# A gated cross-attention block on one core: small per-partition instructions folded together, and a newly written order

## The chip, the cores and the metric

The kernel runs on one core of a Trainium2 chip. The metric is the device time of one execution in microseconds (us). Three executions of the kernel before took 279.45, 279.55 and 279.66 us, median 279.55 us.

The engines go by the names of the profile: PE multiplies matrices (PEld loads its weights), DVE, ACT and POOL work on vectors, and SP issues all the DMAs. Each engine takes its instructions strictly in the order in which the program gives them. An instruction whose input is missing holds up everything behind it on that engine.

## The reference, cut to what matters

Eight batches, x of 256 x 512 each, with a second input (`media`) of the same shape:

```python
x = x + tanh(g_xattn) * xattn(layernorm(x), media)
#   theta = theta_w @ media, phi = phi_w @ x, g = g_w @ x
#   t = softmax(theta.T @ phi) @ g
#   h = relu((t - mean(t)) * rsqrt(var(t) + 1e-5) * gamma + beta), mean and var over a whole batch
#   result: out_w @ h + media
x = x + tanh(g_ffn) * ffn(layernorm(x), w1, w2, w3)
#   bitlinear(a, w): a normalised by its root mean square (eps 1e-6), rounded to 8 bits per row
#                    (scale 127 / max|a|, max|a| at least 1e-5); w rounded to -1, 0, 1
#   h = silu(bitlinear(x, w1)) * bitlinear(x, w2);  result: bitlinear(h, w3)
```

The rows of a batch make two tiles of 128 x 512, so there are 16 feed-forward tiles; tile i belongs to batch i // 2. Each hidden row has 2048 numbers.

## The kernel before, in words

The program first collects 1512 steps, each with a label such as `ug3:0` (kind, part, batch or tile). A list `CFG["order"]` (line 68) then says in which order the steps are issued, and a table `CFG["alt"]` says which engine takes a step that could run on several. So the order on every engine, SP's DMA queue included, is written out in advance. A step waits for its inputs through semaphores, and a tile waits for a free buffer of its pool: 8 banks of PSUM, 31 buffers of 2 KB per partition, 7 of 4 KB and 7 of 8 KB.

The steps that this text speaks of:

- `Lx`, `Lm`, `wl`: loads of x, of media and of the fp32 weights (lines 203, 207, 283). `ws`, `wr`, `wq`: the weights' absolute sum, their scaling to int16 and their clipping to -1, 0, 1 (lines 296 to 321).
- Attention, per batch: `nr`, `np`, `nm`, `nx` normalise x (lines 347 to 352); `jtheta`, `jphi`, `jg` are projections on PE, `htheta`, `hphi` their copies out of PSUM; `sm` the scores, `sx` and `se` their maximum (DVE) and exponential (ACT); `ph`, `pl` split the softmax into two fp16 halves; `pt` transposes it by DMA; `av` multiplies it by g. `tw`, `tm`, `tu`, `td`, `tr`, `tp` make mean and reciprocal deviation of the result (lines 569 to 578). `rm` and `rx` add the media to x ahead of time (lines 444 to 451). `om` is the output projection and `oa` adds it to x, leaving the row sums in `osum` (line 621).
- Entry to the feed-forward part, `ffn_in`, per batch: `im` makes minus the mean out of `osum` (line 651), `iq` squares (ACT), `ir` takes the maximum, `iv`, `ie`, `ip`, `ic` turn these into scales, `iz` quantises x (line 667), `it` transposes the quantised batch by DMA into `fqt` (line 684). `ia`, `ib`, `if` and `ig` write the factors `fback` that take the quantisation back (lines 675 to 682).
- Feed-forward, per tile: `ug` and `uu` multiply `fqt` by w1 and w2, four blocks of four matmuls each (line 699); `us` is SiLU on ACT (line 709), `um` the product on DVE (line 711); `qs` and `qa` take sum of squares and maximum of the hidden row; `qf`, `qm`, `qc`, `qe`, `qr`, `qp`, `qb` are on one number per partition (lines 733 to 740); `qz` quantises the row and `qt` transposes it by DMA into `fhi`; `dm` multiplies by w3 and `da` adds to x. Batches 2 to 6 take a cheaper product of two by two blocks instead of `dm` (`tS`, `tP`, `tU`, `tA`, lines 826 to 897), with sums of weight blocks made once (`tW`).

Which step stands where decides much here. All 16 feed-forward blocks of batch 0 and those of batch 1 use the eight PSUM banks in turn with the attention of later batches, and `ug`/`uu` of batch 1 can't begin before `it:1` has landed.

Of the kernel before, what the change touches and what calls it, by code (L numbers as in the profile page):

```python
# [11 lines left out]
F16 = mybir.dt.float16  # L12
# [77 lines left out]
def flamingo_gated_block(  # L90
# [74 lines left out]


    xs = [[w_(f"x{b}_{c}", [P, T]) for c in range(DC)] for b in range(B)]
    meds = [[w_(f"med{b}_{c}", [P, T]) for c in range(DC)] for b in range(B)]
    proj_w = {n: c_(f"{n}_w", [P, DC, L]) for n in ("theta", "phi", "g")}
    proj_src = {"theta": theta_wT, "phi": phi_wT, "g": g_wT}  # L170

    cols, tg = c_("cols", [P, columns.shape[1]]), c_("tg", [P, 2])
    col = {n: (lambda k=k: cols()[:, k : k + 1]) for k, n in enumerate(("theta", "phi", "g"))}
    ob = lambda: cols()[:, 3 : 3 + DC]
    gates = lambda: cols()[:, 3 + DC : 5 + DC]
    gam, bet, ow = c_("gam", [P, T]), c_("bet", [P, T]), c_("ow", [P, D])
    ones, neg_half = c_("ones", [P, P]), c_("neg_half", [P, 2 * DC])

    fac = {n: (c_(f"{n}_max", [P, DC]), c_(f"{n}_sum", [P, 1]), c_(f"{n}_back", [P, 1]), c_(f"{n}_fwd", [P, 1])) for n in ("phi", "g")}
    half_w = {n: c_(f"{n}_half", [P, 2, DC, L], F16) for n in ("phi", "g")}  # L180
    theta_hi, theta_lo = c_("theta_whi", [P, DC, L], F32R), c_("theta_wlo", [P, DC, L], F32R)
    cols2 = c_("cols2", [P, 2])
    bias = {"theta": (lambda: cols2()[:, 0:1]), "phi": (lambda: cols2()[:, 1:2])}

    whole_x = [b for b in range(B) if b not in CFG["xsplit"]]
    whole_m = [b for b in range(B) if b not in CFG["msplit"]]
    assert set(whole_x) <= set(whole_m)
    keep = {"phi": False, "g": any(b not in CFG["p32"] for b in whole_x), "theta": any(b not in whole_x for b in whole_m)}
    scaled_t = {n: c_(f"{n}_sc", [P, DC, L]) if k else w_(f"{n}_sc", [P, 2 * DC, L]) for n, k in keep.items()}
# [19 lines left out]
    def constants():  # L209
        op("C:ones", lambda: V.memset(ones(), 1.0))  # L210
        op("C:half", lambda: V.memset(neg_half(), -0.5))
        if CFG["p32"] or CFG["rpe"]:
            op("C:id0", lambda: G.memset(ident(), 0.0))
            op(
                "C:id1",
                lambda: G.affine_select(
                    out=ident(), in_=ident(), compare_op=ALU.not_equal, fill=1.0, base=0, pattern=[[-1, P]], channel_multiplier=1
                ),
            )
        wps = ps_("warm")  # L220

        op("C:warm", lambda: [PE.matmul(wps()[:, 0:P], ones(), ones(), start=True, stop=True) for _ in range(CFG["warm"])])
        for n in ("theta", "phi", "g"):
            load_proj(n)
        op("Lc:0", lambda: nc.sync.dma_start(out=cols(), in_=columns))
        op("Lgam:0", lambda: nc.sync.dma_start(out=gam(), in_=ln_gamma))
        op("Lbet:0", lambda: nc.sync.dma_start(out=bet(), in_=ln_beta))
        op("Low:0", lambda: nc.sync.dma_start(out=ow(), in_=out_wT))
        op("C:tanh", lambda: S.activation(tg(), gates(), AF.Tanh))
        if CFG["rpe"]:  # L230
            tiny("C:gid", lambda e: e.tensor_scalar(gident(), ident(), tg()[:, 0:1], 1.0, ALU.mult, ALU.mult))

        tiny("C:ow", lambda e: e.tensor_scalar(ow(), ow(), tg()[:, 0:1], 1.0, ALU.mult, ALU.mult))
        op("C:owh", a=lambda: S.copy(ow_hi(), ow()), v=lambda: V.tensor_copy(ow_hi(), ow()))
        tiny("C:owl", lambda e: e.tensor_tensor(ow_lo(), ow(), ow_hi().bitcast(F32), ALU.subtract))
        tiny("C:ob", lambda e: e.tensor_scalar(ob(), ob(), tg()[:, 0:1], 1.0, ALU.mult, ALU.mult))

        for n in ("phi", "g"):
            mx, sm, back, fwd = fac[n]
            tot = ps_(f"{n}_tot")
            op(f"C:{n}max", lambda n=n, mx=mx: V.tensor_reduce(mx(), proj_w[n](), AX.X, ALU.max, apply_absolute_value=True))
            op(f"C:{n}sum", lambda mx=mx, sm=sm: V.tensor_reduce(sm(), mx(), AX.X, ALU.add))
            op(f"C:{n}tot", lambda sm=sm, tot=tot: PE.matmul(tot()[:, 0:1], ones(), sm(), start=True, stop=True))
            lim = 1e-30 if n == "phi" else 1e-2
            op(f"C:{n}back", lambda tot=tot, back=back, lim=lim: V.tensor_scalar(back(), tot()[:, 0:1], lim, 1.0 / G_SCALE, ALU.max, ALU.mult))
            op(f"C:{n}fwd", lambda back=back, fwd=fwd: V.reciprocal(fwd(), back()))
            tiny(f"C:{n}w", lambda e, n=n, fwd=fwd: e.tensor_scalar(scaled_w[n](), proj_w[n](), fwd(), 1.0, ALU.mult, ALU.mult))  # L250
            op(
                f"C:{n}h",
                a=lambda n=n: S.copy(half_w[n]()[:, 0], scaled_w[n]()),
                v=lambda n=n: V.tensor_copy(half_w[n]()[:, 0], scaled_w[n]()),
            )
            tiny(f"C:{n}l", lambda e, n=n: e.tensor_tensor(half_w[n]()[:, 1], scaled_w[n](), half_w[n]()[:, 0], ALU.subtract))
        pback, pfwd = fac["phi"][2:]
        tiny("C:tw", lambda e: e.tensor_scalar(scaled_w["theta"](), proj_w["theta"](), pback(), 1.0, ALU.mult, ALU.mult))
        tiny("C:tb", lambda e: e.tensor_scalar(cols2()[:, 0:1], col["theta"](), pback(), 1.0, ALU.mult, ALU.mult))
        tiny("C:pb", lambda e: e.tensor_scalar(cols2()[:, 1:2], col["phi"](), pfwd(), 1.0, ALU.mult, ALU.mult))  # L260
        op(
            "C:th",
            a=lambda: S.copy(theta_hi(), scaled_w["theta"]()),
            v=lambda: V.tensor_copy(theta_hi(), scaled_w["theta"]()),
        )
        tiny("C:tl", lambda e: e.tensor_tensor(theta_lo(), scaled_w["theta"](), theta_hi().bitcast(F32), ALU.subtract))
        tiny("C:gback2", lambda e: e.tensor_scalar(gback(), fac["g"][2](), 1.0 / P_SCALE, 1.0, ALU.mult, ALU.mult))
# [4 lines left out]
    def weights(n):  # L272
# [30 lines left out]
        if n < 2:  # L303
            op(f"wf:{n}", lambda: V.tensor_scalar(wfac()[:, n : n + 1], wmean()[:, n : n + 1], 1.0 / (127.0 * Q_UNIT), None, ALU.mult))
        else:
            op(f"wf:{n}", lambda: V.tensor_scalar(wmean()[:, 2:3], wmean()[:, 2:3], tg()[:, 1:2], None, ALU.mult))
# [22 lines left out]
    def attention(b):  # L329
# [215 lines left out]
        for g, pt in enumerate(pts):  # L545
# [14 lines left out]
        op(  # L560
            f"tx:{b}",
            a=lambda: S.activation(tx(), av(), AF.Identity, bias=col["g"](), scale=gb()),
            v=lambda: V.tensor_scalar(tx(), av(), gb(), col["g"](), ALU.mult, ALU.add),
        )
        op(f"tb:{b}", lambda: V.bn_stats(st(), tx()))
        op(f"ta:{b}", lambda: V.bn_aggr(mv2(), st()))
        op(
            f"tw:{b}",
            lambda: V.scalar_tensor_tensor(mv2()[:, 1:2], mv2()[:, 0:1], mv2()[:, 0:1], mv2()[:, 1:2], ALU.mult, ALU.add),
        )  # L570
        op(f"tm:{b}", lambda: PE.matmul(mps()[:, 0:2], ones(), mv2(), start=True, stop=True))
        op(f"tu:{b}", lambda: V.tensor_scalar(mu(), mps()[:, 0:2], 1.0 / P, None, ALU.mult))
        op(
            f"td:{b}",
            lambda: V.scalar_tensor_tensor(var(), mu()[:, 0:1], mu()[:, 0:1], mu()[:, 1:2], ALU.mult, ALU.subtract),
        )
        tiny(f"tr:{b}", lambda e: e.tensor_scalar(rs(), var(), -1.0, LN_EPS, ALU.mult, ALU.add))
        op(f"tp:{b}", lambda: G.tensor_tensor(rs(), rs(), neg_half()[:, 0:1], ALU.pow))
        h = tx
        op(f"hc:{b}", lambda: V.scalar_tensor_tensor(h(), tx(), mu()[:, 0:1], gam(), ALU.subtract, ALU.mult))  # L580
        op(f"hs:{b}", lambda: V.scalar_tensor_tensor(h(), h(), rs(), bet(), ALU.mult, ALU.add))
        if osp:
            hh, hl = w_(f"hh{b}", [P, T], F32R), w_(f"hl{b}", [P, T], F32R)
            op(
# [9 lines left out]
        else:  # L594
# [4 lines left out]
                p=lambda: G.tensor_scalar(h(), h(), 3e38, 0.0, ALU.min, ALU.max),  # L599
            )  # L600

        osums = sums[b] = []
        for c in range(DC):
            o = ps_(f"o_ps{b}_{c}")

# [193 lines left out]


    HC, HT = FC // 2, T // 2
    tw = w_("w3t", [P, 4, HC, HT], F8)

    def block(k, n, q):

# [154 lines left out]
```

## Time and profile before

| | before |
|---|---|
| three runs, median (lowest to highest) | 279.55 us (279.45 to 279.66) |
| the profiled execution: time, and its span from first to last instruction | 279.37 us, 277.6 us |
| granted PE clock, mean | 0.999 |
| PE busy | 271.3 us, 98% of the span |
| DVE, ACT, POOL busy | 254.0, 227.6, 205.9 us (91%, 82%, 74%) |
| DMA | 43.30 MB, mean 156 GB/s |

The span is the stretch that the trace covers; the other 1.8 us of the execution lie around it. A busy share is a mean over stages that differ: in some of them all four compute engines are busy at once. Matmuls overlap in PE, so that a matmul of 512 columns lasts 379 ns by itself but the next can start 216 ns later; a busy PE can still have steps that begin late, and these are found in the view of waits and in the timeline.

### The profile page before, as it was taken

How to read it: one execution, taken by the hardware profiler on the slowest of the kernel's cores; microseconds unless marked ns; L12 is line 12 of the kernel's file. 1: busy time of each engine (PE TensorE's matmuls, PEld its weight loads, DVE VectorE, ACT ScalarE, POOL GpSimd, SP SyncE). 2: the span in 40 equal slices, each digit the busy share in tenths (PEclk: the TensorE clock that was granted, in tenths of full speed). 3: DMA queues.
4: the chain of work that ended last, by engine and by line, in shares of the span. 5: the costliest groups of instructions: out<-in, count | busy, mean ns of one | idle time of the engine just before them, and what ended most of it. 6: DMA issues, size and time to landing. Idle time of an engine off the chain costs nothing.

```text
span 277.6 us, 4741 instructions
## 1 busy us (share of the span) xinstructions
PE 271.3 (98%) x1574; PEld 166.9 (60%) x1574; DVE 254.0 (91%) x537; ACT 227.6 (82%) x337; POOL 205.9 (74%) x273
## 2 busy tenths in 40 slices
PE   7999999999899999999999999999999999999995
PEld 7458585564365555545754778655545566457863
DVE  3798988999999989989999899997999889999895
ACT  1399999999989999899999899895867789675910
POOL 2588774799999998867896989758785855873461
PEclk9999999999999999999999999999999999999999
DMA  7999979998761325134948815916372356605685
GB/s 217 357 347 374 387 277 367 184 195 327 154 115 38 79 41 110 40 76 130 155 97 180 161 41 113 154 34 118 88 142 76 61 130 113 151 2 110 77 211 212
DMA packets 81528, 43.30 MB, mean 156 GB/s; under 512 B 67936, under 2 KB 69088, under 8 KB 81504
## 3 DMA queue, kind: packets, MB, share of 16 engines
q1 hardware_dynamic: 81504, 43.00, 62.2%
q8 instruction: 12, 0.20, 0.3%
q14 instruction: 12, 0.10, 0.1%
HBM read 22.02 MB, written 4.19 MB: 94 GB/s over the span
## 4 chain that ended last, share of the span: by engine, by line
PE 82%; DVE 8%; ACT 3%; issue 2%; DMA 2%; POOL 1%; SPq 0%; POOLq 0%; ACTq 0%
PE fup L699 18%; PE fgp L699 17%; PE dp L857 10%; PE fop L772 6%; PE av L538 4%; PE sc L463 4%; PE phi_ps L385 4%; PE theta_ps L385 3%; PE gx_ps L416 3%; PE tp L498 3%; PE o_ps L610 3%; PE sc L461 3%; PE av L551 3%; DVE nmax L472 2%; DMA med<-in_media 2%
## 5 line engine op out<-in xcount | busy, mean ns | idle before, releaser
L699 PEld LDWEIGHTS <-fqt 128*128 128x128 f16 x512 | 49.0, 99 | 56.8 <-issue 3.2
L699 PE MATMUL fgp<-w1q,fqt 128*128 128x512 f16 x256 | 61.7, 379 | 1.4 <-ACT fh L709 1.4
L699 PE MATMUL fup<-w2q,fqt 128*128 128x512 f16 x256 | 62.3, 379 | 0.0
L709 ACT ACTIVATE fh<-fgp,fback 128x512 f32<-128x512 f32 x64 | 41.1, 687 | 10.4 <-PE fgp L699 8.9
L711 DVE TENSOR_TENSOR fh<-fup,fh 128x512 f32<-128x512 f32 x64 | 42.6, 681 | 2.8 <-PE fup L699 1.6
L732 DVE TENSOR_REDUCE fham<-fh 128x1 f32<-128x2048 f32 x15 | 34.2, 2280 | 0.1
L731 ACT ACTIVATE fhq<-fh 128x2048 bf16<-128x2048 f32 x15 | 28.7, 1913 | 0.4 <-POOL fhfl L733 0.4
L745 ACT ACTIVATE fhq<-fh,fhqs 128x2048 f16<-128x2048 f32 (+1 forms) x14 | 26.6, 1907 | 1.9 <-DVE fhqs L735 1.7
L475 ACT ACTIVATE e<-sc,nmax 128x512 f32<-128x512 f32 x32 | 21.8, 689 | 2.8 <-DVE nmax L472 2.3
L772 PE MATMUL fop<-w3q,fhi 128*128 128x512 fp8e4 (+1 forms) x112 | 22.9, 349 | 0.0
L472 DVE TENSOR_REDUCE nmax<-sc 128x1 f32<-128x512 f32 x32 | 21.6, 681 | 0.7 <-PE sc L463 0.3
L450 POOL TENSOR_TENSOR x<-x,med 128x512 f32<-128x512 f32 x14 | 19.3, 1375 | 3.8 <-ACT med L444 3.7
L519 DVE SCALAR_TENSOR_TENSOR ph<-e,rden,ph 128x512 f16<-128x512 f32 x24 | 17.8, 760 | 0.0
L857 PEld LDWEIGHTS <-fhi 128*128 128x128 f16 x160 | 15.6, 98 | 3.6
L538 PE MATMUL av<-pt,gx 128*128 128x256 f16 x144 | 17.5, 273 | 0.0
L772 PEld LDWEIGHTS <-fhi 128*128 128x128 f16 x112 | 10.6, 98 | 9.3 <-DMA fhi<-fhq 0.4
L538 PEld LDWEIGHTS <-gx 128*128 128x128 f16 x144 | 13.8, 98 | 3.4 <-issue 0.3
L667 POOL TENSOR_SCALAR fq<-x,fnmu,fqs 128x512 f16<-128x512 f32 x16 | 14.1, 889 | 0.8 <-DVE fqs L663 0.2
L654 ACT ACTIVATE fsq<-x,fnmu 128x512 f32<-128x512 f32 x16 | 11.5, 719 | 3.1 <-DVE fnmu L651 2.3
L345 DVE BATCH_NORM_STATS2 bst<-x 128x6 f32<-128x512 f32 x16 | 10.8, 683 | 3.3 <-DMA x<-in_x 3.2
L416 PEld LDWEIGHTS <-xh 128*128 128x128 f16 x144 | 9.4, 98 | 5.5 <-issue 3.3
L621 DVE SCALAR_TENSOR_TENSOR x<-o_ps,x 128x512 f32<-128x512 f32 x16 | 10.9, 687 | 1.9 <-PE o_ps L610 1.6
(223 smaller groups left out, 688.9 us busy)
## 6 DMA issues: line engine op xcount, KB each, us to landing
x<-in_x SPq DMA_DIRECT2D x16, 256.0 KB, 4.0
med<-in_media SPq DMA_DIRECT2D x16, 256.0 KB, 4.5
w<-in_w2T SPq DMA_DIRECT2D x4, 1024.0 KB, 7.7
w<-in_w1T SPq DMA_DIRECT2D x4, 1024.0 KB, 8.2
w<-in_w3T SPq DMA_DIRECT2D x4, 1024.0 KB, 9.7
out<-x SPq DMA_DIRECT2D x15, 256.0 KB, 2.3
fhi<-fhq SPq DMA_TRANSPOSE x17, 4.4
gam<-in_ln_gamma SPq DMA_DIRECT2D x1, 256.0 KB, 10.4
```

What stands on the lines that cost most here:

```text
L385: PE.matmul(ps(), w, v, start=c == 0 and k == 0, stop=c == DC - 1 and k == e)
L472: op(f"sx{t}:{b}", lambda sc=sc, nmax=nmax: V.tensor_reduce(nmax(), sc(), AX.X, ALU.max, negate=True))
L475: lambda t=t, sc=sc, nmax=nmax, e=e: S.activation(e(), sc(), AF.Exp, bias=nmax(), accum_out=den()[:, t : t + 1]),
L538: PE.matmul(av()[:, ts(g, TG * P)], gx()[:, hg, ts(s, L)], v[:, hp, s], start=k == 0, stop=k == 3 * TCH - 1)
L699: PE.matmul(ps(), qt()[:, c * EC + k, :], wq[n][j]()[:, k, :], start=k == 0, stop=k == EC - 1)
L709: lambda j=j, gp=gp: S.activation(h()[:, ts(j, 512)], gp(), AF.Silu, scale=back()[:, c, 0:1]),
L711: op(f"um{j}:{i}", lambda j=j, up=up: V.tensor_tensor(h()[:, ts(j, 512)], up(), h()[:, ts(j, 512)], ALU.mult))
L731: op(f"qs:{i}", lambda: S.activation(hq().bitcast(BF16), h(), AF.Square, accum_out=ss()[:, 0:1]))
L732: op(f"qa:{i}", lambda: V.tensor_reduce(am()[:, 0:1], h(), AX.X, ALU.max, apply_absolute_value=True))
L745: return S.mul(hq()[:, sl], h()[:, sl], qs())
L772: PE.matmul(o()[:, sl], hi()[:, f, :], wq[2][f // 4]()[:, f % 4, sl], start=f == 0, stop=f == FC - 1)
L857: PE.matmul(banks[n]()[:, h * HT : (h + 1) * HT], l()[:, f, :], r(f), start=f == 0, stop=f == HC - 1)
```

## The change

Three things change together.

First, the small instructions. The variance's `tr` goes: `tu` adds 1e-5 to the second moment as it comes out of PSUM, from a constant `eps2`, and `td` subtracts the other way round. The two `osum` tiles of a batch become one with two columns, so that one `im` of two columns takes the place of two of one column. The two `if` become one with broadcast operands. `qf` goes, since its constant is put into `wfac`, the factor of the second weight; `qe` goes, since a new step `ge` of two columns per batch writes that value into a fourth column of `fback`. That is 8 `tr`, 8 `im`, 8 `if`, 16 `qf` and 16 `qe` less, and 8 `ge` and two small fills (`C:e0`, `C:e1`) more: 46 steps fewer, 1466 in all.

Second, `CFG["order"]` and `CFG["alt"]` are new throughout. PE and SP have the same 369 and 105 steps in another order. Between DVE, ACT and POOL, 126 steps change their engine: 48 leave DVE and 52 come to it, 23 leave ACT and 17 come, 55 leave POOL and 57 come. PE now issues all 16 blocks of batch 0 before the first of batch 1, where 13 stood ahead of it. The steps on POOL between `it:0`'s and `it:1`'s quantisation are now `wr1:0, im:1, wr0:0, rm0:2, np:4, rx0:2, rm1:3, ph0:3, ip:1, rm0:3, mh1:5, ic:1, iz0:1, iz1:1`; they were `im0:1, nr:4, ia:0, wr0:0, ib:0, wr1:0, rx0:2, rm1:3, np:4, ip:1, ic:1, iz0:1, iz1:1`.

Third, a second layout of the sums of weight blocks is added, for a setting that neither kernel uses.

```diff
-_upd(CFG, {..., "alt": {...}, "order": [0, 4, 2, 110, ...]})
+_upd(CFG, {..., "alt": {...}, "order": [...]})
...
+        op("C:e0", lambda: G.memset(eps2(), 0.0))
+        op("C:e1", lambda: G.memset(eps2()[:, 1:2], LN_EPS))
...
+            unit = 1.0 / (127.0 * Q_UNIT) / (Q_EPS * RMS_EPS**0.5 if n else 1.0)
+            op(f"wf:{n}", lambda: V.tensor_scalar(wfac()[:, n : n + 1], wmean()[:, n : n + 1], unit, None, ALU.mult))
...
-        op(f"tu:{b}", lambda: V.tensor_scalar(mu(), mps()[:, 0:2], 1.0 / P, None, ALU.mult))
+        op(f"tu:{b}", lambda: V.scalar_tensor_tensor(mu(), mps()[:, 0:2], 1.0 / P, eps2(), ALU.mult, ALU.add))
...
-        tiny(f"tr:{b}", lambda e: e.tensor_scalar(rs(), var(), -1.0, LN_EPS, ALU.mult, ALU.add))
-        op(f"tp:{b}", lambda: G.tensor_tensor(rs(), rs(), neg_half()[:, 0:1], ALU.pow))
+        op(f"tp:{b}", lambda: G.tensor_tensor(rs(), var(), neg_half()[:, 0:1], ALU.pow))
...
+        tiny(f"im:{b}", lambda e: e.tensor_scalar(nmu(), sums[b](), -1.0 / T, 1.0, ALU.mult, ALU.mult))
...
-            tiny(f"im{c}:{b}", lambda e, c=c: e.tensor_scalar(nmu()[:, c : c + 1], sums[b][c](), -1.0 / T, 1.0, ALU.mult, ALU.mult))
...
+        op(
+            f"ge:{b}",
+            lambda: V.scalar_tensor_tensor(
+                back()[:, :, 3], back()[:, :, 2], 1.0 / Q_EPS**2, back()[:, :, 2], ALU.mult, ALU.mult
+            ),
+        )
...
-        tiny(f"qf:{i}", lambda e_: e_.tensor_scalar(fl(), back()[:, c, 2:3], Q_EPS * RMS_EPS**0.5, 1.0, ALU.mult, ALU.mult))
-        op(f"qm:{i}", lambda: V.tensor_scalar(am()[:, 0:1], am()[:, 0:1], fl(), 1.0 / (127.0 * Q_UNIT), ALU.max, ALU.mult))
+        op(f"qm:{i}", lambda: V.tensor_scalar(am()[:, 0:1], am()[:, 0:1], back()[:, c, 2:3], 1.0 / (127.0 * Q_UNIT), ALU.max, ALU.mult))
...
-        tiny(f"qe:{i}", lambda e_: e_.tensor_scalar(e(), back()[:, c, 2:3], back()[:, c, 2:3], RMS_EPS, ALU.mult, ALU.mult))
-        tiny(f"qr:{i}", lambda e_: e_.tensor_scalar(r(), ss()[:, 0:1], 1.0 / FF, e(), ALU.mult, ALU.add))
+        tiny(f"qr:{i}", lambda e_: e_.tensor_scalar(r(), ss()[:, 0:1], 1.0 / FF, back()[:, c, 3:4], ALU.mult, ALU.add))
```

## The prediction

> **What bounds the kernel now.** I read the page's first part, then the busy times by stage, PE's waits, and the timelines of PE, SP and POOL about the only wait of size.
>
> ```profile
> span 277.6 us, 4741 instructions
> PE 271.3 (98%) x1574; PEld 166.9 (60%) x1574; DVE 254.0 (91%) x537; ACT 227.6 (82%) x337; POOL 205.9 (74%) x273
> ```
>
> PE leaves 277.6 − 271.3 = 6.3 us of the span. The stages (columns: stretch, its length, busy us of PE, PEld, DVE, ACT, POOL, clock, DMA share, GB/s) say where:
>
> ```profile
> 0.00:10.00 10.00, 8.34 (x37) 6.26 (x38) 4.32 (x14) 2.17 (x3) 3.46 (x9) 1.00 0.79 246
> 10.00:50.00 40.00, 40.00 (x215) 26.39 (x214) 36.45 (x89) 36.31 (x62) 28.98 (x46) 1.00 1.00 354
> 50.00:75.00 25.00, 23.64 (x126) 12.90 (x124) 24.97 (x58) 24.32 (x38) 22.56 (x25) 1.00 0.89 210
> 75.00:160.00 85.00, 85.00 (x470) 48.78 (x469) 81.28 (x171) 80.90 (x114) 73.04 (x82) 1.00 0.51 104
> 160.00:250.00 90.00, 89.94 (x541) 53.73 (x540) 84.11 (x169) 72.91 (x107) 65.83 (x97) 1.00 0.47 93
> 250.00:277.60 27.60, 24.38 (x198) 18.87 (x195) 22.83 (x43) 10.98 (x17) 12.09 (x17) 0.99 0.67 153
> ```
>
> 1.66 us lie before the first data have landed, 1.36 in 50 to 75 us, 3.22 behind the last matmul, next to nothing elsewhere. The matmuls are the same in number and shape after the change, so head and tail stay and only the middle term can be won. The clock is full.
>
> Waits of PE, its timeline and that of its weight loads and of SP (start, duration, engine, line, operation; in brackets the idle time before and what released it):
>
> ```profile
> PE fgp L699 <- ACT fh L709: 1.4, 1, 1.4
> ```
> ```profile
> 69.69 1.25 SPq L684 DMA_TRANSPOSE fqt<-fq  x1
> 70.65 1.03 PE L699 MATMUL fup<-w2q,fqt 128*128 128x512 f16 x4
> 73.02 0.98 PEld L699 LDWEIGHTS <-fqt 128*128 128x128 f16 x6 [1.84 <-DMA fqt<-fq]
> 73.03 1.25 PE L699 MATMUL fgp<-w1q,fqt 128*128 128x512 f16 x5 [1.35 <-ACT fh L709]
> ```
>
> PE stands from about 71.5 to 73.0, at the first `ug` of batch 1. The matmul's row blames ACT, but the weight load is released by the landing of `it:1`, issued at 69.69; the eight such transposes land 3.0 to 3.3 us after issue, so at 72.7 to 73.0. PE comes 1.5 us too early for it. What made `it:1` late is on POOL:
>
> ```profile
> 56.82 1.97 POOL L313 TENSOR_SCALAR w1q<-w,wscale 128x2048 int16<-128x2048 f32 x1
> 58.75 0.69 POOL L676 TENSOR_TENSOR fam<-fam,fr 128x2 f32<-128x2 f32 x1
> 59.43 2.40 POOL L313 TENSOR_SCALAR w1q<-w,wscale 128x2048 int16<-128x2048 f32 x1
> 61.80 1.83 POOL L450 TENSOR_TENSOR x<-x,med 128x512 f32<-128x512 f32 x1
> 63.61 1.27 POOL L445 TENSOR_SCALAR med<-med,tg,cols 128x512 f32<-128x512 f32 x1
> 64.85 1.27 POOL L348 TENSOR_TENSOR rstd<-rstd,neg_half 128x2 f32<-128x2 f32 x1
> 65.54 1.52 POOL L662 TENSOR_TENSOR fr<-fz,neg_half 128x4 f32<-128x4 f32 x1
> 67.15 0.38 POOL L663 TENSOR_SCALAR fqs<-fr 128x2 f32<-128x2 f32 x1
> 67.64 2.03 POOL L667 TENSOR_SCALAR fq<-x,fnmu,fqs 128x512 f16<-128x512 f32 x2
> ```
>
> These are `wr0:0, ib:0, wr1:0, rx0:2, rm1:3, np:4, ip:1, ic:1` and both `iz` of batch 1: POOL works without a break from 56 us to 69.7 us.
>
> **The instructions removed.** On POOL, by its groups: `im` 8 × 0.32, `if` 9 × 0.48, `qf` 12 × 0.19, `qe` 11 × 0.47, `tr` 6 × 0.47, some 17 us by the page's durations (which overlap), less the four `im` and five `if` of two columns that remain there: about 13 us. On DVE, `im` 8 × 0.15, `if` 7 × 0.32, `qe` 5 × 0.20 and the like, less what stays and eight new `ge` (nearest row `td`, 0.33): about 2 us. None is on PE, which is the bound in every stage, so by themselves they are worth nothing; PE's full 85.0 and 89.94 us of work cover them. Without that cover DVE's 2 us would be its worth. `tu` with a tensor of constants costs a tenth of a us at most, eight times, under the same cover. The two fills of `eps2` stand in the head while POOL has 3.46 us of work in 10. Their only effect on the end can go through the order.
>
> **The order, at the one hole.** Two things move.
> PE issues all 16 blocks of batch 0 first, where 13 were ahead: 3 blocks × 4 matmuls × 0.216 = 2.59 us more, so PE reaches `ug` of batch 1 at 71.5 + 2.6 = 74.1. They were issued later before, so this adds nothing to PE's sum; the hole stays equal if `it:1` lands 2.59 later, at 75.6, and closes if it lands by 74.1.
> POOL, between the two quantisations, loses `nr:4` (0.19), `ia` (0.20), `ib` (0.69), and gains `rm0:2`, `rm0:3` (0.92 in quiet stretches, 1.27 here), `ph0:3` (0.69 quiet, 1.08 crowded) and `mh1:5` (0.62): 3.15 to 4.24 us. The two `im0:1`, `im1:1` become one. Net +2.07 to +3.16. `iz1:1` then ends at 71.7 to 72.8 and, with the present 3.2 from there to the landing (69.7 to 72.9), lands at 74.9 to 76.0. Against 75.6 the hole changes by −0.7 to +0.4. Batch 0's and 1's squares on ACT come some 0.3 later by the sum of ACT's work ahead of them; I add it once. The centre is −0.15 + 0.3, near zero: hole about 1.5 us, time as before.
> Which end holds depends on crowding: the nine rows above take about 3 us more than the same forms at their shortest (`wr` 2.40 against 1.97, `rx` 1.83 against 1.28, `rm` 1.27 against 0.92, `np` 1.27 against 0.71, `ip` 1.52 against 1.02, `iz` 1.02 against 0.77 each, ...). I take the row of this stretch, since DVE's and ACT's load in it stays.
>
> A rule stands against putting steps on POOL here. The Trainium skill, "SBUF — State Buffer", section "Who interferes with whom", says that DVE in its fast modes, or with two SBUF inputs, locks a pair of ports that GpSimd also needs, for a whole instruction. By the rule each of seven weight casts of DVE in the stretch (0.68 us each) could hold POOL for its full length, 4.8 us where the rows show about 3; `it:1` would then land near 76.9, and the time be about 1.3 us above before. The rows decide the sum above.
>
> **The order elsewhere.** Two casts of `phi` go from ACT to DVE in the head, and the second copy of the weights' sums comes behind all eight absolute sums: ACT is 96% busy from 10 to 75 us with or without, and a slip of half a us at the first softmax falls into the same hole. The first normalisations of batch 0 go to POOL, which has 6.5 us free there. ACT crosses between exponential and SiLU eight times, as before (a table load is 1.28 us in ACT's rows), so no term. Between 75 and 250 us each DMA transpose must land before PE comes to it; the tightest I find is `qt:2`. It had 7.0 us of PE's work behind it before `dm0:2`; now `dm0:2` stands next. PE reaches it at 114.4 + 2.0 = 116.4. On POOL `qz:2` stands behind `tW00`, `im:3` and `tW01`; `im:3`, now one instruction, waits for both `oa` of batch 3, about 105.5, with `tW01` and `qz:2` queued behind it: 105.5 + 0.3 + 2.0 + 1.9 = 109.7; issue 110, and 4.75 from issue to landing as at 103.5 before, makes 114.6. So 1.8 us of margin, priced at nothing; each us beyond costs one.
>
> **The sum.** 279.37 us of the profiled execution (277.6 span, 1.8 around it; 0.18 below the median) + 0 for the small instructions + 0.15 for the hole, −1.5 to +0.4 with bounds: 279.5.
>
> **Rivals.** *No change (forecast), 0.36*: the hole moves behind the sixteenth block and keeps its size. Own range 278.9 to 280.3. For it: the two shifts are nearly equal. Against: both are sums of crowded rows.
>
> *Faster: the hole closes, 0.29.* With 15 us less of little instructions, POOL's chain might run near its shortest durations: 3 us less over the stretch puts the landing at 72 to 73.5, before PE's 74.1. All 1.5 us goes: 278.0, or 278.9 where part stays. More can't be won, since no other hole is there. Against: DVE's casts, which go with the crowding, stay.
>
> *Slower: `im:3` holds up `qz:2`, 0.24.* If `oa` of batch 3 or the `tW` on POOL slip by over 1.8 us, PE stands at `dm0:2`. POOL lost about 3 us to crowding in 56 to 70 us; a slip of 3.4 gives 1.6 us: 281.1. For it: `tW` takes 2.0 to 2.34, and the wait is new. Against: POOL is less loaded there.
>
> *Other places in an order written anew, 0.11*: DVE is 95% busy from 75 to 160 us, and a wait of PE in any of its turns of eight banks comes at 1:1; 280.3 to 282.
>
> *That the change doesn't do what it says:* the algebra moves factors only, so it is whole; if the small instructions don't matter at all, that is the forecast.
>
> **Numbers.** Some 0.2% (0.56 us) is about what a measurement of this kernel can tell from no change. Faster by more: 0.29 and 0.04 of the forecast's lower tail, 0.33. Within: 0.27. Slower: 0.24 + 0.11 + 0.05 = 0.40. The range 278.2 to 281.6 leaves out about 0.06 below and 0.13 above. Cases of both signs hold most of the chance; the likeliest alone is 278.9 to 280.3.
>
> **What would show it.** Right: PE busy still 271.3; one wait of 0.8 to 1.9 us at the first `ug` of batch 1, near 74 to 76, released by `fqt`; `it:1` issued at 71.7 to 72.8; POOL's busy time down by over 10 us with the span unchanged. The faster rival: no wait there, and `iz1:1` done by 71. The slower: a wait at L772 near 116, with `fhi` as releaser. Wrong altogether: a wait of PE over 0.5 us at any other line, a tail over 3.7 us, or a first matmul later than 6.5 us.

## The result, and the profile after

The changed kernel is slower: 281.12 us median of 4 runs (280.50 to 281.23) against 279.61 for before, a ratio of 1.0048 (95% interval 1.0029 to 1.0066); run again, 280.78 us, 1.0037 (1.0023 to 1.0051). By the ratios that is 1.0 to 1.3 us. The profiled execution took 280.50 us with a span of 278.4: 0.8 us more span than before, and 2.1 us around it instead of 1.8. Slow executions are left out of the times below, and the profiles of `after_wq1_act` and `after_casts`, which fell in slow ones at a granted clock of 0.85 and 0.95, are not used.

The first part of the page, three stages (PE, PEld, DVE, ACT, POOL busy, clock, DMA share, GB/s), and PE's waits:

```profile
span 278.4 us, 4688 instructions
PE 271.7 (98%) x1574; PEld 166.5 (60%) x1574; DVE 253.6 (91%) x530; ACT 221.8 (80%) x331; POOL 196.5 (71%) x239
```
```profile
10.00:50.00 40.00, 40.00 (x208) 25.88 (x207) 36.39 (x94) 36.55 (x63) 29.71 (x41) 1.00 0.98 353
50.00:75.00 25.00, 23.85 (x128) 12.77 (x127) 24.88 (x60) 23.24 (x38) 20.81 (x22) 1.00 0.81 200
75.00:160.00 85.00, 84.39 (x470) 47.98 (x469) 83.45 (x162) 79.86 (x111) 71.05 (x77) 1.00 0.48 100
```
```profile
PE fgp L713 <- DMA fqt<-fq: 0.6, 1, 0.6
PE fup L713 <- DVE mu L576: 0.6, 1, 0.6
PE fgp L713 <- DVE w1q L325: 0.5, 1, 0.5
```

POOL is 9.4 us less busy and ACT 5.8, and nothing came of it. PE's one wait of 1.51 us has become three, measured from matmul start to start: 0.63 us at `ug1:1` (64.2 us; a cast of weights on DVE is late), 0.75 at `uu3:0` (73.9; `tu:2` on DVE is late and holds a PSUM bank) and 0.77 at `ug3:2`, the first block of batch 1 (76.4; `it:1`). That block starts at 76.40. Before, it started at 73.03 with three blocks (2.59 us) less ahead of it, so the shift is 76.40 − 75.62 = 0.78 us. From there to the last matmul both kernels take the same time to 0.01 us, with the three blocks counted. The whole growth of the span is made before 76.4 us.

The chain of waits (start, length, what) passes through it:

```profile
59.24 1.78 DVE w1q L325
61.88 2.28 DVE w1q L325 x2
70.44 2.67 POOL fq L670 x2
73.13 3.22 DMA fqt<-fq
76.40 2.76 PE fgp L713 x12
```

DVE stands ahead of POOL in it. The groups of DVE's casts of w1, before (L321) and after (L325), have the same form and count (busy us, mean ns of one, idle time ahead):

```profile
L321 DVE TENSOR_SCALAR w1q<-w1q 128x2048 f16<-128x2048 int16 x4 | 2.6, 681 | 0.0
```
```profile
L325 DVE TENSOR_SCALAR w1q<-w1q 128x2048 f16<-128x2048 int16 x4 | 4.9, 1241 | 0.0
```

DVE stands idle ahead of none of them (0.0): the 2.3 us more are inside the instructions. The timelines of POOL and DVE after show what holds them:

```profile
58.01 2.46 POOL L317 TENSOR_SCALAR w1q<-w,wscale 128x2048 int16<-128x2048 f32 x1
62.31 1.29 POOL L454 TENSOR_TENSOR x<-x,med 128x512 f32<-128x512 f32 x1
65.80 0.69 POOL L518 TENSOR_SCALAR ph<-e,rden 128x512 f16<-128x512 f32 x1 [1.00 <-ACT e L479]
66.64 1.76 POOL L665 TENSOR_TENSOR fr<-fz,neg_half 128x4 f32<-128x4 f32 x1 [0.16 <-DVE fz L664]
70.44 2.65 POOL L670 TENSOR_SCALAR fq<-x,fnmu,fqs 128x512 f16<-128x512 f32 x2
```
```profile
59.16 1.87 DVE L325 TENSOR_SCALAR w1q<-w1q 128x2048 f16<-128x2048 int16 x1
61.80 2.35 DVE L325 TENSOR_SCALAR w1q<-w1q 128x2048 f16<-128x2048 int16 x2
65.48 0.15 DVE L512 RECIPROCAL rden<-rden 128x2 f32<-128x2 f32 x1
```

`wq3:0` starts at 59.16 while POOL's `wr0:0` runs (to 60.47) and ends 0.55 us behind it. `wq1:0`, the second of the pair, starts at 62.40, behind the start of `rx0:2` (62.31 to 63.60), and ends at 64.15, again 0.55 behind. Each would take 0.68. An instruction that so stands until one of the other engine has ended is called held from here on. So DVE loses 1.19 + 1.07 = 2.3 us, `pr0:3` and `ie:1` come late, and POOL waits 1.00 us ahead of `ph0:3` and 0.16 ahead of `ip:1`. The first wait is put down to ACT, but `ph0:3` needs only `se0:3`, long done at 61.45, and `pr0:3`, which ends at 65.63.

### The profile page after: what moved, and what is told of

Same layout as the page of the kernel before. It is cut to its first block, busy times and chain, and to the rows that moved or that the text cites. A ratio compares the mean times of both kernels' runs of the same rounds, so it can differ in the third digit from the quotient of the medians.

```text
span 278.4 us, 4688 instructions
## 1 busy us (share of the span) xinstructions
PE 271.7 (98%) x1574; PEld 166.5 (60%) x1574; DVE 253.6 (91%) x530; ACT 221.8 (80%) x331; POOL 196.5 (71%) x239
## 4 chain that ended last, share of the span: by engine, by line
PE 77%; DVE 11%; ACT 4%; DMA 3%; issue 2%; POOL 2%; SPq 0%; POOLq 0%
PE fgp L713 17%; PE fup L713 16%; PE dp L871 11%; PE fop L784 6%; PE phi_ps L389 4%; PE sc L467 4%; PE theta_ps L389 4%; PE av L542 3%; PE gx_ps L420 3%; PE tp L502 3%; PE av L555 3%; PE o_ps L615 2%; PE sc L465 2%; DVE nmax L476 2%; DMA med<-in_media 2%
## 5 line engine op out<-in xcount | busy, mean ns | idle before, releaser
L713 PE MATMUL fgp<-w1q,fqt 128*128 128x512 f16 x256 | 61.0, 379 | 1.1 <-DMA fqt<-fq 0.6
L757 ACT ACTIVATE fhq<-fh,fhqs 128x2048 f16<-128x2048 f32 (+1 forms) x12 | 22.7, 1896 | 1.1 <-DVE fhqs L748 1.1
L454 POOL TENSOR_TENSOR x<-x,med 128x512 f32<-128x512 f32 x11 | 14.5, 1320 | 0.5 <-DVE med L450 0.4
L583 POOL TENSOR_TENSOR rs<-var,neg_half 128x1 f32<-128x1 f32 x8 | 6.8, 849 | 11.3 <-DVE var L579 11.2
L670 POOL TENSOR_SCALAR fq<-x,fnmu,fqs 128x512 f16<-128x512 f32 x15 | 12.5, 841 | 1.8 <-DVE fqs L666 1.2
L665 POOL TENSOR_TENSOR fr<-fz,neg_half 128x4 f32<-128x4 f32 x8 | 10.0, 1254 | 4.4 <-DVE fz L664 4.3
L356 POOL TENSOR_SCALAR xn<-x,nmu,rstd 128x512 f32<-128x512 f32 x15 | 12.6, 840 | 0.4
```

What stands on the lines that cost most here:

```text
L713: PE.matmul(ps(), qt()[:, c * EC + k, :], wq[n][j]()[:, k, :], start=k == 0, stop=k == EC - 1)
L757: return S.mul(hq()[:, sl], h()[:, sl], qs())
```

## The experiments

The first matmul with data starts between 6.0 and 7.2 us, by chance of the first loads; where positions of two profiles are compared, that difference is taken off.

**Order or algebra.** Four runs. The first is the changed kernel without an edit.

> The changed kernel once more, as the base of the other runs. Both theories: 280.5 to 281.3 us, and the wait of PE at the first ug of batch 1 between 0.5 and 1.5 us. Theory A (the new order costs, by POOL's chain before it:1): whatever the total is, the time of this profile against before follows the landing of it:1 one to one. Theory B (the algebra costs, its new forms of instruction): no bound on where PE waits.

280.78 us. Its profile has the same three waits (0.80, 0.78, 0.77 us).

```diff
 # alg_only: the changed code, the order and engines of before
-"order": [the new one]
+"order": [that of before; im behind the later oa, if at the first if, ge behind ig]
```

> The algebra of the change in the order of before (the removed steps left out, im and if at the place of the earlier of their pair, ge behind ig). Theory A (the order costs): 279.2 to 279.8 us, with the wait of PE at ug of batch 1 still 1.2 to 1.7 us, since POOL loses only one small im ahead of it:1. Theory B (the algebra costs): 280.5 to 281.2 us.

285.83 us, ratio 1.0228 (1.0210 to 1.0245): both theories failed, the order of before doesn't bear the new steps at all. What happens at 57 us is shown further on.

```diff
 # order_only: the code of before, the order and engines of the changed kernel
+"order": [the new one; im0, im1 for im; if0, if1 for if; tr before tp; qf before qm; qe before qr]
```

> The order and the engines of the changed kernel with the algebra of before (im0 and im1, if0 and if1, tr, qf, qe put back beside their successors, ge and the two fills gone). Theory A (the order costs): 280.8 to 281.6 us, the wait at ug of batch 1 as in the changed kernel or 0.2 to 0.3 longer for one more im on POOL. Theory B (the algebra costs): 279.3 to 280.0 us.

281.73 us, 1.0077 (1.0059 to 1.0094), with 0.85 us of wait at `ug3:2`. So the new order loses without the new algebra too, and within it the algebra is worth about 0.004, some 1 us; in the old order the same algebra costs 0.0228.

```diff
 # after_iz_early, on POOL
-ph0:3  ip:1  rm0:3  mh1:5  ic:1  iz0:1  iz1:1
+ip:1  ic:1  iz0:1  iz1:1  ph0:3  rm0:3  mh1:5
```

> The changed kernel with ph0:3, rm0:3 and mh1:5 behind iz1:1 on POOL instead of ahead of ip:1. Theory A (POOL's chain before it:1 sets the end): it:1 is issued at 70.4 to 71.2 instead of 73.1, lands at 73.6 to 74.4, the wait for it (0.77 us in the changed kernel's profile) is gone and the time 0.5 to 0.9 us below the changed kernel; no more than that, as PE's two waits for DVE before it (0.63 and 0.75 us) stay. Theory C (those two waits for DVE set the end by themselves, and it:1 only lies behind them): the time stays within 0.2 us of the changed kernel.

280.73 us, 1.0044 (1.0028 to 1.0061): no gain. `it:1` was issued at 71.71, the wait for it went, and PE stood at `om0:2` instead, 0.9 us at 80.8 us:

```profile
PE o_ps L615 <- DVE hl L597: 0.7, 1, 0.7
```

So theory A is right that the wait goes and wrong about what it is worth; the total is theory C's, within 0.2 us of the changed kernel, though not for its reason. Inside the span this version is even slower, 278.9 us against 278.65 in the median, and spends 0.3 us less outside it. A second chain, DVE's to `hl:2`, ends where POOL's chain to `it:1` ends.

**Who holds whom.** In the run of the algebra alone, DVE's `im:1` of two columns met `wr0:0` on POOL (the rows: DVE, then POOL):

```profile
57.21 1.67 DVE L652 TENSOR_SCALAR fnmu<-osum 128x2 f32<-128x2 f32 x1
...
56.89 1.97 POOL L317 TENSOR_SCALAR w1q<-w,wscale 128x2048 int16<-128x2048 f32 x1
```

Before, `im1:1` of one column started beside the same `wr0:0` and took 0.14:

```profile
56.84 0.14 DVE L651 TENSOR_SCALAR fnmu<-osum 128x1 f32<-128x1 f32 x1
```

```diff
 # alg_split; alg_split2 does the like with ge
-tensor_scalar(nmu(), sums(), -1/T, 1.0, mult, mult)
+tensor_scalar(nmu()[:, c:c+1], sums()[:, c:c+1], -1/T, 1.0, mult, mult)   # for c in 0, 1
```

> The algebra alone in the order of before, as in the run of the algebra alone (285.8 us), but im issues two instructions of one column instead of one of two columns. Theory H (an instruction of DVE that reads or writes two columns is held until POOL's running instruction ends, one of one column is not): im:1 on DVE takes 0.2 to 0.35 us instead of 1.67, im:3 the like instead of 1.29; the wait of PE for w1q at ug3:0 (1.57 us) falls below 0.4, and the time to 282.5 to 284.6 us. Theory M (the merged im costs because it waits for both row sums, whatever its form): im:1 and im:3 end as late as before, the time stays at 285.3 to 286.3 us.

284.22 us, 1.0179 (1.0152 to 1.0205). `im:1` took 0.20 us and `im:3` 0.27 (two instructions each) and the time lies in theory H's range, but PE's wait at `ug3:0` stayed at 1.57 where H had it below 0.4: the hold went on to the next instruction that can be held, the pair of casts behind it (2 × 0.68 alone).

```profile
58.85 0.20 DVE L652 TENSOR_SCALAR fnmu<-osum 128x1 f32<-128x1 f32 x2
60.76 4.08 DVE L325 TENSOR_SCALAR w1q<-w1q 128x2048 f16<-128x2048 int16 x2
```

> As the run before it, and ge too as two one-column instructions with one tensor operand each (ge:1 took 1.30 and ge:2 1.18 us on DVE with the algebra alone, elsewhere 0.15). Theory H: ge takes 0.25 to 0.4 everywhere, and the time falls by another 0.5 to 2.5 us, to 280.5 to 283.5. Theory M: no change from the run before it, within 0.3 us.

284.48 us, 1.0179 again: `ge` took 0.33 us everywhere, and nothing was gained. Here theory M's number came out, though not for its reason.

```diff
 # after_wq1_act
-wq1:0 on DVE
+wq1:0 on ACT, behind iq1:1, where ACT stood idle for 1.40 us
```

> The changed kernel with one cast of weights, wq1:0, on ACT behind iq1:1 (ACT stands idle there for 1.4 us) instead of on DVE, where it took 1.75 us, held until POOL's rx0:2 ended, instead of 0.68. Theory H (the holds on DVE make pr0:3 and ie:1 late, POOL waits 1.16 us for these, and it:1 is late by that): POOL's wait ahead of ph0:3 falls from 1.0 to below 0.4 us, it:1 is issued 0.5 to 1.2 us earlier, and PE's wait at ug3:2 falls from 0.77 to below 0.3; the time is 0.4 to 0.8 us under the changed kernel if nothing behind is late in its turn, else about the same with a new wait between 76 and 82 us. Theory W (POOL's work alone made it:1 late): it:1 moves by less than 0.3 us.

280.09 us (the next expectation's 280.15 counts one execution of 315.87 us too), 1.0023 (1.0006 to 1.0040). The same kernel again, for a profile:

> The kernel with wq1:0 on ACT once more, for a profile at the full clock (the first one was taken at 0.85 and can't be laid beside the others; its other times had a median of 280.15 us). Theory H (holds on DVE made it:1 late): 279.7 to 280.5 us, POOL's wait ahead of ph0:3 below 0.4 us, it:1 issued 0.5 to 1.2 us earlier than the changed kernel's 73.13, PE's wait at ug3:2 below 0.3 us. Theory W (POOL's work alone): it:1 within 0.3 us of the changed kernel's, counted from the first matmul with data.

279.83 us, 1.0008 (0.9997 to 1.0020): no difference from the kernel before that these runs can tell. The rows on POOL and SP, and what is left of PE's waits:

```profile
64.69 0.69 POOL L518 TENSOR_SCALAR ph<-e,rden 128x512 f16<-128x512 f32 x1 [0.24 <-ACT fsq L657]
65.75 1.76 POOL L665 TENSOR_TENSOR fr<-fz,neg_half 128x4 f32<-128x4 f32 x1 [0.38 <-DVE fz L664]
```
```profile
72.24 1.24 SPq L698 DMA_TRANSPOSE fqt<-fq  x1
```
```profile
PE fgp L713 <- ACT fh L723: 0.4, 1, 0.4
PE fgp L713 <- DMA fqt<-fq: 0.3, 1, 0.3
PE fgp L713 <- ACT w1q L324: 0.3, 1, 0.3
```

POOL's wait ahead of `ph0:3` fell from 1.00 to 0.24 us (that ahead of `ip:1` grew from 0.16 to 0.38), and `it:1` was issued 0.89 us earlier, 0.70 with the earlier first matmul taken off. PE's wait at `ug3:2` fell from 0.77 to 0.48 us, not below 0.3. One cast off DVE takes back most of the change's loss (1.0008 and 1.0023 against 1.0037 and 1.0048). In the run of 1.0008 all that is left lies outside the span: the span is 277.7 us in the median, that of the kernel before beside it 277.9. The edit removes 0.68 us of work from DVE as well as 1.07 of hold; the last runs take these apart.

**The same in the kernel before.** Three edits of it.

```diff
 # before_iz_early
-im0:1 ... wr0:0  ib:0  wr1:0  rx0:2  rm1:3  np:4  ip:1  ic:1  iz0:1  iz1:1     (POOL; iv:1 on DVE)
+im0:1 ... wr0:0  ib:0  wr1:0  iv:1  ip:1  ic:1  iz0:1  iz1:1  rx0:2  rm1:3  np:4
 # on DVE: ie:1 directly behind ir1:1;  on SP: it:1 directly behind it:0, ahead of six loads
```

> The kernel before, with ib:0, wr1:0, iv:1 (on POOL now), ie:1, ip:1, ic:1, both iz and it of batch 1 moved up to stand behind ir1:1, so that rx0:2, rm1:3 and np:4 come after them on POOL. If the landing of it:1 is all that holds PE: it:1 is issued at 65.5 to 67 us instead of 69.7, the wait of 1.51 us at ug of batch 1 is gone and the time is 278.0 to 278.6 us. If POOL and DVE bound the whole stage from 50 to 80 us, and the place of the wait is only where PE meets them: PE waits 0.7 us or more at another step by 82 us, and the time is 279.0 us or more.

283.01 us, 1.0128 (1.0067 to 1.0189). `it:1` was issued at 66.38, its wait was gone, and PE then stood 3.7 us at `av1:3` for a transpose. On SP the edit had put `it:1` ahead of six loads, which before were issued from 57.25 to 60.2 us. Now they came behind it, from 67.71 us, and the two of 1 MB stood just ahead of a transpose, which took 9.8 us to issue instead of about 2:

```profile
66.38 1.23 SPq L684 DMA_TRANSPOSE fqt<-fq  x1
71.32 0.98 SPq L284 DMA_DIRECT2D w<-in_w3T  x2
72.35 9.82 SPq L525 DMA_TRANSPOSE pt<-ph  x1
```

Before, the two loads of weights stood well ahead of `it:1`:

```profile
59.31 0.93 SPq L284 DMA_DIRECT2D w<-in_w3T  x2
```

So this run doesn't tell what POOL's new order alone is worth. The next expectation blames a buffer of media that `rx0:2` frees late. The record doesn't bear that out: before, all six loads were issued before `rx0:2` began at 61.80.

```diff
 # before_iz2: as above, with rx0:2 left ahead of iv:1, and wq2:1, wq3:1, tb:2 ahead of ie:1 on DVE; SP's order as before
```

> The kernel before with iv:1 on POOL, and iv, ie, ip, ic and iz of batch 1 directly behind rx0:2 on POOL, so that only rm1:3 and np:4 come after them; the casts wq2:1 and wq3:1 and tb:2 ahead of ie:1 on DVE; SP's order as before. Moving rx0:2 too had freed a buffer of media late, SP's loads of w3 came late and the transposes behind them took 9.8 us to issue. If that was the cause of that run's loss and the landing of it:1 is the only hold on PE here: it:1 is issued at 67 to 68.5 us, PE's wait of 1.51 us falls below 0.4, time 278.0 to 279.0 us. If POOL and DVE bound the stage as a whole: PE waits at another step by 85 us and the time is 279.2 us or more.

280.12 us, 1.0015 (1.0004 to 1.0026). `wq2:1` was now held (1.77 us), so `ip:1` came only 0.3 us earlier; the wait at `ug` of batch 1 fell to 0.64, and 0.75 appeared at `uu3:0`. Neither edit won time out of the 1.51 us of before by moving POOL's steps; the first of them says little, for SP's order.

```diff
 # before_nudge, on DVE behind wc:0
+5 tensor_scalar of one column
```

> The kernel before with five more one-column instructions on DVE behind wc:0, 0.06 to 0.07 us each, so that DVE is about 0.33 us later from 55 us on; nothing else is changed. Theory R (which of DVE and POOL starts first decides who holds the other: in the kernel before, wq2:0 and wq3:0 of 0.68 us each just got ahead of ib:0 and wr1:0): POOL's ib:0 and wr1:0 get ahead, one of the casts takes 1.2 to 2.5 us instead of 0.68, and the time goes up by 0.8 to 3 us, to 280.3 to 282.6. Theory S (a shift costs at most its size, and PE's wait of 1.51 us takes it up): 279.3 to 279.9 us.

280.57 us, 1.0032 (1.0020 to 1.0045). The five took 0.89 us instead of 0.33, and DVE was 0.81 us late by 55 us. The casts at 59 us kept their 0.68 each, against theory R, but the cast behind them was held:

```profile
62.27 1.72 DVE L326 TENSOR_SCALAR w2q<-w2q 128x2048 f16<-128x2048 int16 x1
```

In return `iv:1` and `ie:1` behind it took 0.16 and 0.15 us instead of 1.24 and 0.59, so the hold changed its place and not its sum. R's time came out, not its reason. The span, counted from the first matmul with data, is 0.80 us longer, so the open 1.51 us took nothing up, against theory S: what DVE was late in this stage, the end was late.

**Work or hold.** Three edits that leave all work on DVE and POOL:

```diff
 # after_mh, on POOL
-ip:1  rm0:3  mh1:5  ic:1  iz0:1  iz1:1  tp:2
+ip:1  rm0:3  ic:1  iz0:1  iz1:1  mh1:5  tp:2
 # after_casts, on DVE
-wq3:0  wf:0  ia:0  tb:2  wf:1  ib:0  wq2:0  wq1:0  sx3:3  if:0 ... ie:1
+wq3:0  wq2:0  wq1:0  wf:0  tb:2  wf:1  sx3:3 ... ie:1  ia:0  ib:0  if:0
```

> The changed kernel with mh1:5 alone behind iz1:1 on POOL, where POOL stands idle for 1.1 us ahead of tp:2. Theory A (POOL's chain before it:1 sets the end): it:1 is issued about 1.0 us earlier than in the changed kernel, PE's wait at ug3:2 (0.77 us) is gone, nothing behind is later as mh1:5 fits into the idle time, and the time is 0.5 to 0.9 us under the changed kernel (280.0 to 280.4). Theory C (the stage as a whole is bound by DVE and POOL): the time stays within 0.25 us of the changed kernel and the wait comes again by 82 us.

280.99 us, 1.0064 (1.0048 to 1.0080), no gain, and by the ratio rather a loss against the changed kernel: the wait at `ug3:2` was gone and 0.63 us stood at `om0:2`, for `hl:2` on DVE, as theory C has it.

> The changed kernel with another order on DVE between 60 and 66 us: wq2:0 and wq1:0 directly behind wq3:0, so that both are through before POOL's rx0:2 begins, and ia:0, ib:0 and if:0 behind ie:1. Nothing changes its engine. Theory H (the hold of wq1:0 by rx0:2, 1.07 us, is what made pr0:3, ie:1 and so it:1 late): wq1:0 takes 0.7 to 1.0 us, PE's wait at ug1:1 (0.63 us) is gone, it:1 is issued 0.7 to 1.2 us earlier, and the time is 0.6 to 1.1 us under the changed kernel, 279.7 to 280.3. Rival (the time saved with wq1:0 on ACT was the DVE work saved, not the hold): it:1 moves by less than 0.3 us and the time by less than 0.3.

281.22 us, 1.0067 (1.0050 to 1.0084), no gain. Theory H's time failed; without a usable profile, where `it:1` went isn't known.

> Both edits together: the casts before rx0:2 on DVE, and mh1:5 behind iz1:1 on POOL. If both waits come from POOL's chain and the hold: it:1 is issued 1.6 to 2.2 us earlier than in the changed kernel, PE waits no more than 0.4 us for it, and the time is 279.0 to 279.6, at or under the kernel before. If DVE's late tu:2 then holds PE at uu3:0: a wait of 0.5 us or more there, and the time 279.6 to 280.0.

281.08 us, 1.0065 (1.0048 to 1.0081); neither expectation came out. Its profile shows why: `wq1:0` took 0.68 as planned, and POOL's `rm0:2` was held by the casts instead, 2.23 us in place of 1.19:

```profile
59.58 3.22 DVE L325 TENSOR_SCALAR w1q<-w1q 128x2048 f16<-128x2048 int16 x3
```
```profile
61.04 2.23 POOL L449 TENSOR_SCALAR med<-med,tg,cols 128x512 f32<-128x512 f32 x1
```

`rx0:2` was 1.0 us later against the first matmul, and ACT's `iq0:1`, which starts when `rx0:2` ends, with it. DVE gained nothing either: `pd0:3` took 1.18 us instead of 0.16.

```diff
 # after_mh_rx
-mh1:5 ahead of ic:1; rx1:2 on DVE
+mh1:5 behind nx1:4; rx1:2 on POOL behind iz1:1
 # after_mh_rx_wq: and wq1:0 on ACT
```

> The changed kernel with mh1:5 behind nx1:4 on POOL, and rx1:2 (1.10 us on DVE, 0.44 of it held) on POOL behind iz1:1 instead of on DVE. Theory D (two chains end together in this stage, POOL's to it:1 and DVE's to hl:2, so that only easing both moves the end; with mh1:5 alone PE's wait only went on from ug3:2 to om0:2): both waits are below 0.3 us, hl:2 ends 0.7 to 1.1 us earlier against the first matmul with data, and the time is 0.5 to 1.2 us under the changed kernel, a ratio to the kernel before of 0.999 to 1.003. Theory P (DVE and POOL bound the stage by the sum of their work, since one holds the other): what goes from DVE to POOL gains nothing, a ratio of 1.004 to 1.0065, as the changed kernel and the kernel with mh1:5 alone.

280.81 us, 1.0054 (1.0038 to 1.0069). DVE was 1.02 us ahead at 69 us, until the new `ge:0` met `rx1:2` on POOL and lost 1.08:

```profile
72.99 1.23 DVE L693 SCALAR_TENSOR_TENSOR fback<-fback 128x2 f32<-128x2 f32 x1
```
```profile
72.49 1.70 POOL L454 TENSOR_TENSOR x<-x,med 128x512 f32<-128x512 f32 x1
```

> As the run before it, and wq1:0 on ACT behind iq1:1 too, which by itself gave a ratio of 1.0008. Theory D: the gains add up, a ratio of 0.996 to 0.999, 278.5 to 279.4 us, under both kernels; what is left of PE's waits is then that for w1q at ug1:1 and the SiLUs behind iq0:1 (0.4 to 0.6 us each). Theory P: 1.000 to 1.002, as with wq1:0 on ACT alone.

280.10 us, 1.0019 (1.0007 to 1.0030), as with the cast on ACT alone. Theory P's numbers came out in both: the work that went from DVE to POOL, or an overlap that was moved, gained nothing; the one cast that left the two of them for ACT did. No version tried passes the kernel before.

## Why the prediction was wrong

*The head, the tail, the clock, and everything behind 76 us* were right: PE's time from `ug` of batch 1 to its last matmul differs by 0.01 us between the kernels. *The slower rival* named 281.1 us, and 281.12 was measured, but that is luck: PE shows no wait at `dm0:2`, `qt:2`'s margin held, and the time was lost 40 us earlier.

*The hole.* The working had it move behind the sixteenth block and keep its size, with +0.15 us and bounds of −1.5 and +0.4. The three waits are 2.15 us together, and the first block of batch 1 starts 0.78 us later than with a hole of the old size. The step that failed is POOL's stretch between the two quantisations. Its work was sized right: 16.13 us instead of 13.77, +2.36 where +2.07 to +3.16 stood. What was missing is 1.16 us in which POOL waits for DVE: the sum took POOL as gap-free after the change because it was so before, and asked of no added step what it waits for. `ph0:3` needs `pr0:3`, and DVE was late for that. So `it:1` was issued 3.44 us later (69.69 to 73.13: 2.36 of work and 1.16 of waiting, from a start 0.09 earlier), 0.85 more than the 2.59 of PE's three blocks; it landed in 0.07 less, and 0.78 is left. PE also came to this block at 75.63 and not at 74.1, for the two new waits ahead of it, which the working didn't have. They cost nothing by themselves here, as the landing came later still.

*Crowding* was counted on one side only: the sum kept POOL's crowded rows and left out what DVE loses. From batch 0's first `oa` to the end of `hl:2`, DVE takes 30.4 us before (48.1 to 78.5) and 31.9 after (48.3 to 80.25). Five instructions are held in the one (`iv:1` 1.24, `ie:1` 0.59, `td:2` 0.66, `if1:0` 0.70, `ib:1` 1.22, some 3.6 us over their length elsewhere), six in the other (`wq3:0` 1.87, `wq1:0` 1.75, `rx1:2` 1.10, `pl2:3` 1.09, `pl3:3` 1.19, `hl:2` 1.75, some 4.6 us over). That difference of 1 us is the larger part of the 1.5. POOL's own losses didn't fall for it: in its stretch between the quantisations its instructions take 4.2 us over the shortest of their form, 3.8 before.

The prediction weighed a rule on this and decided against it. The Trainium skill, "SBUF — State Buffer", section "Who interferes with whom", also says: "Issue order, not op shape, decides who blocks", a half of the rule that the working left out. Part of the traces agrees: `wq1:0` started 0.09 us behind `rx0:2` and was held 1.07 us, and in `after_casts_mh` `wq3:0` came ahead of `rm0:2` and POOL was held 1.04. Part doesn't: there `wq2:0` and `wq1:0` started 0.48 and 1.08 us behind `rm0:2`, while it was still held, and took their 0.68 us all the same. The order of the recorded starts alone doesn't say who is held. The rule's sum, +1.3, is near the measured 1.0 to 1.3, but by luck: it had POOL as the loser, and it counted seven casts where the rows between 56 and 69.7 us have six, which by its own working makes +0.6.

*The faster rival* didn't come, and where an edit closed or narrowed the wait for `it:1`, PE stood elsewhere for DVE within 6 us: 0.9 and 0.63 us at `om0:2` (`after_iz_early`, `after_mh`), 0.75 at `uu3:0` (`before_iz2`). *DVE's* load was weighed only for 75 to 160 us, though the row of 50 to 75 us has it at 24.97 of 25. Two slips changed nothing: ACT's rows give 93% from 10 to 75 us, not 96, and 110 + 4.75 is 114.75, a margin of 1.65 us for `qt:2`.

*The small instructions* were priced at nothing, with DVE's 2 us as the bound if the cover were gone, and about 13 us of POOL; POOL's busy time fell by 9.4. In the new order they are worth about 1 us (`order_only` against the changed kernel, on one chip), and in the old one their replacement costs 6.2. Part of that is shown: `im` waits for both row sums, `im` and `ge` of two columns can be held (1.67 and 1.30 us), and a DVE that comes later is held in other places (`before_nudge`). How much belongs to each isn't settled: undoing the form of `im` won about 1.4 us by the ratios, of `ge` nothing.

*Outside the span* the changed kernel spends 0.3 us more in every run (2.1 against 1.8 us). Nothing in the profile shows what. It is 2.1 in all variants that have both the new order and the new algebra but one (`after_iz_early`, 1.8), and 1.8 with either alone. It stays open, and makes 0.3 of the 1.1 us by which the profiled executions differ.

## What to carry to other kernels

Where DVE and POOL are both nearly full (24.88 and 20.81 of 25 us from 50 to 75 us here), count them as one resource in that stage: find the instructions that are longer than the same form elsewhere, see whose they are, and ask of a new order who will be held. In these runs moving a hold from one of them to the other gained nothing. Ask of each step that is put into a chain what it waits for. A hole in PE names the wait that ended last, not the bound; before pricing its closing, look at which chain ends next behind it. Instructions that are off the critical path by their duration can still decide the time by being held, or by what they make late.

## What the runs showed of the hardware

Over sixteen profiles, 758 one-column and 368 two-column TENSOR_SCALAR instructions of DVE in fp32: none of the first took over 0.28 us, 25 of the second took over 0.35, up to 1.67. No RECIPROCAL of two columns took over 0.17 us (320), while 49 of 256 SCALAR_TENSOR_TENSOR of one column took over 0.35. In the same sixteen profiles 55 instructions of DVE with one to four columns of fp32 in and out took over 0.6 us, and every one ended 3 to 28 ns behind the end of a POOL instruction. So merging two TENSOR_SCALAR of one column into one of two, as `im` does here, saves an issue and makes the result one that can be held.
